# Layer 3 of a hybrid network on one core: attention, two norms and gate logits as one pipeline of four-tile groups

## The chip, the cores and the metric

The kernel runs on one core of a Trainium2 chip. The metric is the device time of one execution in microseconds (us). Over 10 runs the kernel before took a median of 14244.46 us (14234.97 to 14262.62).

The engines are named as in the profile: PE multiplies matrices (PEld loads its stationary operand), DVE is the vector engine, ACT the scalar engine with its function tables, POOL the GpSimd engine, SP the engine that issues most of the transfers. Each engine executes its own queue in order; SP and ACT also issue transfers, in the same queue as their other work.

## The reference, cut to what matters

The network has four layers on an input of 2 x 64 x 64 x 128 (8192 tokens of 128 channels, in float32). Layers 0 to 2 (selective scan, deformable convolution, gated scan with a spectral convolution) aren't touched. Layer 3 is, with x of shape (2, 4096, 128):

```python
# attention, on the layer-normed x
h = layernorm(x)
q = exp(h @ Wq + bq); k = exp(h @ Wk + bk); v = h @ Wv + bv
x = x + q @ (k.T @ v)                    # one 128 x 128 product per batch entry
# mixture of experts, experts choose tokens
n = layernorm(x)
logits = n @ gate_w.T + gate_b           # 64 experts
p = softmax(logits over the tokens)      # per batch entry and expert
g = p where it is among the 8 largest of its row, else 0
xw = g.T @ n                             # one mixed token per batch entry and expert
y = gelu(xw @ weight1 + b1) @ weight2 + b2
x = x + g @ y
```

It is written here as the kernel computes it; what matters is the order: one norm, an attention whose 128 x 128 product needs all the tokens of a batch entry, a second norm, logits, a softmax and a choice of eight over all 4096 tokens, the experts' two large weights (64 x 128 x 512 each, 16.8 MB apiece), and the result added to x.

## The kernel before

The tokens lie in `X`, 64 tiles of 128 tokens (partitions) by 128 channels; each of the two batch entries has 32 tiles (`NTB`). Layer 2 writes its result to HBM, and `move` (L1691) loads it into `X` in eight transfers. Then `layer3a` and `layer3f` run, one after the other.

`layer3a` does for each batch entry:
- `layernorm` (L99): `bn_stats` and `bn_aggr` for 32 tiles on DVE (L107, L108); one reciprocal square root for all 32 (`rsqrt`, L77: a square root on ACT at L82 and six small DVE operations); then tile by tile the normalised copy, in turn on DVE (L121) and ACT (L119), and its transpose on PE into PSUM (L95), copied to `xt` by DVE (L72) and ACT (L74) in turn.
- `pq` (L1529) and its exponential into `qt` (L1530), `pkv` (L1535) with bias (L1537) and exponential (L1538), the product `kvp` over all tiles (L1540) and its copy `kvs` (L1542).
- `po` (L1546), added to `X` (L1548).

`layer3f` loads the first four pieces of the experts' first weight (`w1`, L1569, 2 MB each, on SP's queue), normalises `X` a second time into a copy `xn3` of its own, transposes it, and forms the logits of both batch entries as the sum of two zero-padded products in one PSUM tile (L1592), so that partition 64 b + e holds expert e of batch entry b. The whole row of 4096 logits is then searched for its eight largest values (`max`, L1595), these are overwritten (`match_replace`, L1596), the exponential and its sum are taken (L1600), and in eight pieces the chosen places are found (L1604) and the weighted values put into `G` (L1605). `G` is transposed (L95) into `gt`, and `pp` (L1612) forms the mixed tokens, copied to `xw` (L1613). Only after that are `b1`, `b2`, `sel8` and `sel2` loaded, on ACT's queue (L1617 to L1624), and on SP's queue the first three pieces of the second weight (`w2`). The expert loop goes over eight groups of eight experts: `ph` (L1644), a copy, `phid` with the selector `sel8` (L1648), bias and GELU (L1650, L1652), `pout` with `w2` (L1657), `poe` with the selector `sel2` (L1663). The last part multiplies by `G` (`py`, L1675), adds `X` (L1677) and stores.

The order of each engine's queue in layer 3 isn't written out: the framework's planner sorts the instructions, by the order in which they are written and by the time at which it believes their operands ready, so that work of the second batch entry can slip between work of the first. (Layer 2 has an order written by hand.) A buffer is reused when all its readers are done; a new pool lies where an earlier one lay, and its first writers wait for that memory's last readers.

Of the kernel before, what the change touches and what calls it, by code (L numbers as in the profile page):

```python
# [96 lines left out]


def layernorm(k, pool, ps, t0, n, tag, xn=None, xt=None):  # L99


    nc = k.nc
    st = pool.tile([P, n, 6], F32, name=f"{tag}_st", tag=f"{tag}_st")
    mv = pool.tile([P, n, 2], F32, name=f"{tag}_mv", tag=f"{tag}_mv")
    rs = pool.tile([P, n], F32, name=f"{tag}_rs", tag=f"{tag}_rs")
    for i in range(n):
        nc.vector.bn_stats(st[:, i, :], k.X[:, t0 + i, :])  # L107
        nc.vector.bn_aggr(mv[:, i, :], st[:, i, :])  # L108
    rsqrt(nc, pool, rs, mv[:, :, 1], 1e-5, [P, n], tag)
    sh = pool.tile([P, n], F32, name=f"{tag}_sh", tag=f"{tag}_sh")  # L110
    nc.vector.scalar_tensor_tensor(sh, mv[:, :, 0], -1.0, rs, ALU.mult, ALU.mult)

    def normalised(i):
        if xn is not None:
            o = xn[:, i, :]
        else:
            o = pool.tile([P, C], F32, name=f"{tag}_n", tag=f"{tag}_n", bufs=6)
        if i % 2:
            nc.scalar.activation(o, k.X[:, t0 + i, :], AF.Identity, bias=sh[:, i : i + 1], scale=rs[:, i : i + 1])  # L119
        else:  # L120
            nc.vector.tensor_scalar(o, k.X[:, t0 + i, :], mv[:, i, 0:1], rs[:, i : i + 1], ALU.subtract, ALU.mult)  # L121
        return o

    if xt is None:
        for i in range(n):
            normalised(i)
    else:
        to_channels(k, ps, xt, normalised, n)
# [1379 lines left out]
def layer3a(k):  # L1508
    tc, nc, ins, X = k.tc, k.nc, k.ins, k.X
    with ExitStack() as es:  # L1510
        enter = es.enter_context
        cst = enter(tc.tile_pool(name="a3c", bufs=1))
        pool = enter(tc.tile_pool(name="a3p", bufs=2))
        wk = enter(tc.tile_pool(name="a3w", bufs=4))
        ps = enter(tc.tile_pool(name="a3ps", bufs=6, space=PSUM))
        pk = enter(tc.tile_pool(name="a3pk", bufs=2, space=PSUM))
        wq = cst.tile([P, C], F32, name="wq")
        nc.sync.dma_start(out=wq, in_=ins["wq3"])
        wkv = cst.tile([P, 2, C], F32, name="wkv")
        nc.sync.dma_start(out=wkv[:, 0, :], in_=ins["wk3"])  # L1520
        nc.sync.dma_start(out=wkv[:, 1, :], in_=ins["wv3"])
        for b in range(B):
            xt = pool.tile([P, L], F32, name="xt3")
            layernorm(k, pool, ps, b * NTB, NTB, "ln3", xt=xt)
            qt = pool.tile([P, L], F32, name="qt")
            for q in range(8):
                s = slice(q * N, (q + 1) * N)
                pq = ps.tile([P, N], F32, name="pq3", tag="ps")
                nc.tensor.matmul(pq, wq, xt[:, s], start=True, stop=True)  # L1529
                nc.scalar.activation(qt[:, s], pq, AF.Exp, bias=k.v("bq"))  # L1530
            kvp = pk.tile([P, C], F32, name="kvp")
            for i in range(0, NTB, 2):
                pkv = ps.tile([P, 2, 2 * C], F32, name="pkv", tag="ps")
                for j in range(2):
                    nc.tensor.matmul(pkv[:, j, :], xt[:, (i + j) * P : (i + j + 1) * P], wkv.rearrange("p a c -> p (a c)"), start=True, stop=True)  # L1535
                kv = wk.tile([P, 2, 2 * C], F32, name="kv")
# [12 lines left out]

def layer3f(k, out):


# [307 lines left out]
```

## Time and profile before

| | us |
|---|---|
| median of 10 runs | 14244.46 |
| the profiled execution, its own time | 14250.63 |
| its span | 14248.9 |
| layer 3: first `bn_stats` to the end of the span | 13945.7 to 14248.9 |
| of this: first `bn_stats` to the first transposition | 13945.7 to 13958.4 |
| first `kvs` to second `kvs` | 13996.9 to 14043.1 |
| last logits out of PSUM | 14084.0 |
| `pp`, 128 matmuls | 14109.7 to 14137.1 |
| wait of PE for `sel8` | 14143.8 to 14153.8 |
| `py` | 14230.0 to 14244.5 |

The profile's time for one execution lies 6.17 us above the median of the runs, so times read from the profile are used as differences. Over the whole span the page has DVE busy for 90%, POOL for 86%, PE for 81% and ACT for 64%; almost all of that is layers 0 to 2. In layer 3 no engine is busy throughout, and each stage has another limit, so the tables by stage say more than the page's shares. "PEclk" is the clock that PE was granted, 1.00 being full speed.

### The profile page before, as it was taken

To read this page: it belongs to the slowest core of one execution; us is meant where nothing else is said; L and a number is where in the kernel's file an instruction comes from. 1 tells how busy PE (TensorE), PEld (TensorE's weight loads), DVE (VectorE), ACT (ScalarE), POOL (GpSimd) and SP (SyncE) were. 2 spreads that over 40 slices of the span, in tenths; PEclk is the share of its full clock that TensorE was granted. 3 is DMA by queue.
4 is the path that set the end of the run, shared out by engine and by line. 5 is a ranking of instruction groups with operands and counts; after the bars stand their busy time and mean duration, and the time that the engine had idled before them with its cause. 6 is when DMAs were issued, how large, how long until landed. Compare 5 with 4: busy or idle time off the path is not lost. (4 is left out here: it accounts for less than half of the span.)

```text
span 14248.9 us, 234505 instructions
## 1 busy us (share of the span) xinstructions
PE 11537.0 (81%) x91784; PEld 7492.7 (53%) x91784; DVE 12780.6 (90%) x11825; ACT 9132.5 (64%) x15238; POOL 12199.8 (86%) x3232
## 2 busy tenths in 40 slices
PE   7888788887895464979869798797887989989997
PEld 4444544445883132646536465564454656656665
DVE  7889678896658999999999999999999999999953
ACT  5777367772115676777767667667777777777742
POOL 5888358882778999999999999999999999999950
PEclk9999799998996676989879899898998999999998
DMA  7999679996974454656656565565665666666653
GB/s 180 228 226 231 174 169 230 229 230 172 285 213 153 151 175 155 214 186 206 196 172 206 187 203 202 191 204 187 205 202 185 208 196 206 208 199 205 210 150 133
DMA packets 1388836, 2800.92 MB, mean 197 GB/s; under 512 B 375985, under 2 KB 1046353, under 8 KB 1184721
## 3 DMA queue, kind: packets, MB, share of 16 engines
q1 hardware_dynamic: 1192560, 1556.57, 41.5%
q10 hardware_dynamic: 148608, 1076.17, 20.9%
q0 software_dynamic: 46560, 153.18, 3.6%
q8 instruction: 724, 11.86, 0.4%
q14 instruction: 384, 3.14, 0.1%
HBM read 2364.15 MB, written 421.31 MB: 195 GB/s over the span
## 5 line engine op out<-in xcount | busy, mean ns | idle before, releaser
L1462 DVE TENSOR_TENSOR_SCAN S<-dA,S 128x512 f32<-128x512 f32 x8192 | 9155.0, 1195 | 123.4 <-ACT dA L1460 97.5
L1406 POOL TENSOR_TENSOR S<-row,g 128x4088 f32<-128x4088 f32 (+1 forms) x1024 | 9058.9, 8897 | 182.8 <-DMA row<-drow 114.4
L1460 ACT ACTIVATE dA<-row,a_t 128x512 f32<-128x512 f32 x8192 | 5632.2, 692 | 2491.3 <-DVE S L1462 2396.1
L1425 PE MATMUL Z<-S,cv 128*32 128x256 f32 x32768 | 2568.1, 445 | 1633.1 <-ACT ze L1430 1288.2
L1264 PE MATMUL pef<-hk,ur 128*128 128x256 f32 x14336 | 3550.6, 388 | 18.4 <-DMA hk<-in_phi_dram 12.7
L1264 PEld LDWEIGHTS pef<-hk,ur 128*128 128x128 f32 x14336 | 2630.1, 191 | 973.1 <-issue 628.6
L404 POOL TENSOR_TENSOR S<-row,bt 128x2048 f32<-128x2048 f32 x512 | 2318.4, 4529 | 353.4 <-DMA row<-drow 285.4
L1425 PEld LDWEIGHTS Z<-S,cv 128*32 128x32 f32 x32768 | 1029.7, 123 | 2873.2 <-issue 1411.0
L502 DVE TENSOR_TENSOR_SCAN S<-dA,S 128x1024 f32<-128x1024 f32 x1024 | 2282.6, 2272 | 100.4 <-POOL S L410 82.6
L424 PE MATMUL dA<-dt,quad 64*128 64x255 f32 x8192 | 1251.8, 431 | 420.9 <-DVE S L502 379.6
L438 ACT ACTIVATE dA<-dA 128x1020 f32<-128x1020 f32 x1024 | 1022.5, 1003 | 344.8 <-PE dA L424 280.7
L424 PEld LDWEIGHTS dA<-dt,quad 64*128 64x128 f32 x8192 | 784.0, 203 | 868.9 <-DVE S L502 525.4
L1264 PEld LDWEIGHTS pef<-hd,ur 128*128 128x128 f32 x4096 | 752.2, 191 | 302.6 <-issue 196.0
L1264 PE MATMUL pef<-hd,ur 128*128 128x256 f32 (+1 forms) x4096 | 861.6, 335 | 5.8 <-ACT e L1244 3.1
L1236 PE MATMUL acc<-e,mw 128*128 128x512 f32 x1600 | 855.9, 618 | 5.6 <-ACT e L1244 4.5
L779 POOL DMA_INDIRECT G<-table,idx x576 | 553.9, 962 | 219.0 <-issue 141.3
L456 PE MATMUL Z<-S,W 128*32 128x128 f32 x16384 | 658.7, 294 | 101.4 <-ACT ze L462 87.8
L1430 ACT COPY ze<-Z 128x512 f32<-128x512 f32 x1024 | 591.6, 578 | 166.1 <-PE Z L1425 135.6
L456 PEld LDWEIGHTS Z<-S,W 128*32 128x32 f32 x16384 | 432.2, 116 | 393.8 <-issue 187.7
L787 DVE TENSOR_TENSOR G<-G,wv 128x1536 f32<-128x1536 f32 x192 | 335.9, 1751 | 271.2 <-DMA G<-table,idx 254.7
L1244 ACT COPY e<-pef 128x512 f32<-128x512 f32 x800 | 464.7, 581 | 167.9 <-PE acc L1236 106.1
L791 PE MATMUL pv<-ident,G 128*128 128x128 f32 x4608 | 534.7, 278 | 2.8 <-DVE G L787 2.8
(344 smaller groups left out, 7407.0 us busy)
## 6 DMA issues: line engine op xcount, KB each, us to landing
row<-drow ACTq DMA_DIRECT2D x1024, 1024.0 KB, 5.4
row<-drow SPq DMA_DIRECT2D x512, 1024.0 KB, 12.7
zd<-ze SPq DMA_DIRECT2D x1024, 256.0 KB, 2.7
hk<-in_phi_dram SPq DMA_DIRECT2D x224, 320.5 KB, 4.4
hk<-in_phi_dram SPq DMA_DIRECT2D x160, 448.5 KB, 5.1
hd<-in_phi_dram SPq DMA_DIRECT2D x512, 128.5 KB, 4.4
hk<-in_phi_dram SPq DMA_DIRECT2D x96, 576.5 KB, 6.1
mw<-wdr SPq DMA_DIRECT2D x400, 128.0 KB, 3.1
```

Of the source, the lines that this page charges most:

```text
L404: nc.gpsimd.tensor_tensor(S[:, o, :], rows.pop(s), bt[:, 0, sub * T : (sub + 1) * T].unsqueeze(1).to_broadcast([P, 8, T]), ALU.mult)
L424: nc.tensor.matmul(dA[:, 2 * a + h, rest], stats[d, j][r, h, :], dt[r, h, at : at + T - 1], start=True, stop=True)
L438: nc.scalar.activation(dA[:, :, rest], dA[:, :, rest], AF.Exp)
L456: nc.tensor.matmul(Z[32 * q : 32 * q + 32, :, :, a].rearrange("p t g -> p g t"), w, S[:, :, t : t + 4], start=True, stop=True)
L502: nc.vector.tensor_tensor_scan(flat, dflat, flat, 0.0, ALU.mult, ALU.add)
L1236: nc.tensor.matmul(box["acc"].rearrange("p a s -> p (a s)"), ms[f][:, o, :], e, start=box["first"], stop="whole" in box and (f, o) == todo ...
L1264: nc.tensor.matmul(pe[:, a, 256 - n :], ur[:, par, j, :], h[:, at : at + n], start=i == 0, stop=i + 1 == len(mm))
L1406: nc.gpsimd.tensor_tensor(S, row[:, :, first:].unsqueeze(1).to_broadcast([P, 2, R, T - first]), g[:, :, first:].unsqueeze(2).to_broadcast( ...
L1425: nc.tensor.matmul(Z[32 * j : 32 * j + 32, q].rearrange("p t e -> p e t"), cv[:, h, s], S[:, h, :, s], start=h == 0, stop=h == 1)
L1430: nc.scalar.copy(ze, Z)
L1460: nc.scalar.activation(dA, row[:, j % R, :], AF.Exp, scale=a_t[:, h, d : d + 1])
L1462: nc.vector.tensor_tensor_scan(s, dA, s, 0.0, ALU.mult, ALU.add)
```

## The change

`layer3a`, `layer3f` and the helper `layernorm` are replaced by one function `layer3`, called in their place.

- Statistics are taken for a group of four tiles (`stats`): four `bn_stats` and four `bn_aggr` on DVE, and the reciprocal square root by fourteen operations on POOL with one exponential of the bit pattern on ACT between the first and the second, in place of the square root on ACT and six DVE operations for 32 tiles. `mv3` and `vs3` keep mean, rsqrt, square root and shift of all 64 tiles for one norm at a time.
- `transposed` normalises and transposes one group; all copies out of PSUM are ACT's. The first norm, `pq`, `pkv` and `kvp` follow group by group, with `kvp` one group behind.
- The second norm is written over `X` itself, group by group behind `po`; the copy `xn3` is gone. The first batch entry's transposed tiles are kept in `G`'s memory. POOL undoes the norm in the expert loop (`X = X * sqrt(var) + mean`, one operation a tile).
- Logits use two groups of 64 columns of PE, one for each batch entry, in place of two padded products that are added. They and a `max` of each group of 512 follow the transposes of the second batch entry.
- The exponential (ACT) is issued beside `match_replace` (DVE); marking and weighting are one operation a piece, without the sum; the reciprocal of the sum goes into the matrix `big_r` by which `G` is transposed (a float32 matmul, no longer a transposition), and into `oe`.
- `b1`, `b2`, `sel8` and the gate weight are loaded at the start of the layer, on ACT's queue, with the attention's weights. `w1`'s four pieces are loaded during the first batch entry. `sel2` is loaded behind the first three pieces of `w2`.

```diff
+def layer3(k, out):
+    NE, EG, HF, Q = 64, 8, 512, 4
+    NQ = NTB // Q
...
+        wq = cst.tile([P, C], F32, name="wq")
+        nc.scalar.dma_start(out=wq, in_=ins["wq3"])
...
+        gw = cst.tile([P, NE], F32, name="gw")
+        nc.scalar.dma_start(out=gw, in_=ins["gate_w"])
...
+        sel8 = cst.tile([P, 8], F32, name="sel8")
+        nc.scalar.dma_start(out=sel8, in_=ins["sel8"])
+        big_r = cst.tile([P, P], F32, name="big_r")
+        mv = cst.tile([P, NT, 2], F32, name="mv3")
+        vs = cst.tile([P, NT, 4], F32, name="vs3")
+        w1 = {}
         with ExitStack() as e2:
             pre = e2.enter_context(tc.tile_pool(name="m3p", bufs=1))
+            wk = e2.enter_context(tc.tile_pool(name="m3wk", bufs=4))
             ps = e2.enter_context(tc.tile_pool(name="m3ps", bufs=6, space=PSUM))
+            pa = e2.enter_context(tc.tile_pool(name="m3pa", bufs=2, space=PSUM))
+            def stats(q):
+                st = wk.tile([P, Q, 6], F32, name="st3")
+                i = slice(q * Q, q * Q + Q)
+                for j in range(Q):
+                    nc.vector.bn_stats(st[:, j, :], X[:, q * Q + j, :])
+                for j in range(Q):
+                    nc.vector.bn_aggr(mv[:, q * Q + j, :], st[:, j, :])
+                va, r, t, m = (vs[:, i, n] for n in range(4))
+                g = nc.gpsimd
+                g.tensor_scalar(va, mv[:, i, 1], 1e-5, None, ALU.add)
+                nc.scalar.activation(r, va.bitcast(I32), AF.Exp, scale=-0.5 * LN2 / 2**23, bias=root[:, 0:1])
+                g.tensor_tensor(t, va, r, ALU.mult)
+                g.tensor_tensor(t, t, r, ALU.mult)
+                g.tensor_scalar(m, t, 0.375, -1.25, ALU.mult, ALU.add)
+                g.tensor_tensor(m, t, m, ALU.mult)
+                g.tensor_scalar(m, m, 1.875, None, ALU.add)
+                g.tensor_tensor(r, r, m, ALU.mult)
+                g.tensor_tensor(t, va, r, ALU.mult)
+                g.tensor_tensor(t, t, r, ALU.mult)
+                g.tensor_scalar(t, t, -0.5, 1.5, ALU.mult, ALU.add)
+                g.tensor_tensor(r, r, t, ALU.mult)
+                g.tensor_tensor(m, mv[:, i, 0], r, ALU.mult)
+                g.tensor_scalar(m, m, -1.0, None, ALU.mult)
+                g.tensor_tensor(t, va, r, ALU.mult)
+            def transposed(q, keep, out):
+                pt = ps.tile([P, N], F32, name="pt", tag="ps")
+                for j in range(Q):
+                    i = q * Q + j
+                    o = X[:, i, :] if keep else wk.tile([P, C], F32, name="xn3", bufs=6)
+                    if j % 2:
+                        nc.vector.tensor_scalar(o, X[:, i, :], mv[:, i, 0:1], vs[:, i, 1:2], ALU.subtract, ALU.mult)
+                    else:
+                        nc.scalar.activation(o, X[:, i, :], AF.Identity, bias=vs[:, i, 3:4], scale=vs[:, i, 1:2])
+                    nc.tensor.transpose(pt[:, j * P : (j + 1) * P], o, k.ident)
+                nc.scalar.copy(out, pt)
+            lg = pre.tile([P, L], F32, name="lg")
+            G = cst.tile([P, L], F32, name="G3")
+            xt4 = G
+            m64 = pre.tile([P, NQ, 8], F32, name="m64")
+            def logits(q, xt):
+                pl = ps.tile([P, N], F32, name="pl", tag="ps")
+                for b, t in enumerate((xt4[:, q * N : (q + 1) * N], xt)):
+                    nc.tensor.matmul(pl[b * NE : (b + 1) * NE, :], gw, t, start=True, stop=True)
+                s = lg[:, q * N : (q + 1) * N]
+                nc.scalar.activation(s, pl, AF.Identity, bias=k.v("gate_b"))
+                nc.vector.max(m64[:, q, :], s)
             for b in range(B):
+                at = b * NQ
+                qt = pre.tile([P, L], F32, name="qt", tag="big", bufs=2)
+                kvp = pa.tile([P, C], F32, name="kvp")
+                behind = []
+                def products():
+                    while behind:
+                        q, j, kv = behind.pop(0)
+                        for h in range(2):
+                            nc.tensor.matmul(kvp, kv[:, h, :C], kv[:, h, C:], start=q == j == h == 0, stop=q == NQ - 1 and j == h == 1)
+                stats(at)
+                for q in range(NQ):
+                    if q + 1 < NQ:
+                        stats(at + q + 1)
+                    xt = wk.tile([P, N], F32, name="xt3")
+                    transposed(at + q, False, xt)
+                    pq = ps.tile([P, N], F32, name="pq3", tag="ps")
+                    nc.tensor.matmul(pq, wq, xt, start=True, stop=True)
+                    nc.scalar.activation(qt[:, q * N : (q + 1) * N], pq, AF.Exp, bias=k.v("bq"))
+                    products()
+                    for j in range(2):
+                        pkv = ps.tile([P, 2, 2 * C], F32, name="pkv", tag="ps")
+                        for h in range(2):
+                            s = slice((2 * j + h) * P, (2 * j + h + 1) * P)
+                            nc.tensor.matmul(pkv[:, h, :], xt[:, s], wkv.rearrange("p a c -> p (a c)"), start=True, stop=True)
+                        kv = wk.tile([P, 2, 2 * C], F32, name="kv")
+                        nc.vector.tensor_tensor(kv, pkv, k.r("bkv").unsqueeze(1).to_broadcast([P, 2, 2 * C]), ALU.add)
+                        nc.scalar.activation(kv[:, :, :C], kv[:, :, :C], AF.Exp)
+                        behind.append((q, j, kv))
+                    if b == 0:
+                        w1[q // 2] = w1.get(q // 2) or load(wp1, "w1", q // 2)
+                products()
+                kvs = wk.tile([P, C], F32, name="kvs", bufs=2)
+                nc.vector.tensor_copy(kvs, kvp)
+                def normalised(q):
+                    if b == 0:
+                        transposed(at + q, True, xt4[:, q * N : (q + 1) * N])
+                    else:
+                        xt = wk.tile([P, N], F32, name="xt3")
+                        transposed(at + q, True, xt)
+                        logits(q, xt)
+                for q in range(NQ):
+                    po = ps.tile([P, N], F32, name="po4", tag="ps")
+                    for j in range(Q):
+                        i = q * Q + j
+                        nc.tensor.matmul(po[:, j * P : (j + 1) * P], qt[:, i * P : (i + 1) * P], kvs, start=True, stop=True)
+                    o = X[:, (at + q) * Q : (at + q + 1) * Q, :]
+                    nc.vector.tensor_tensor(o, po.rearrange("p (a c) -> p a c", c=C), o, ALU.add)
+                    stats(at + q)
+                    if q > 0:
+                        normalised(q - 1)
+                normalised(NQ - 1)
+            m8 = pre.tile([P, 8], F32, name="m8")
+            nc.vector.max(m8, m64.rearrange("p a b -> p (a b)"))
+            sm = cst.tile([P, 4], F32, name="sm3")
+            nc.vector.tensor_scalar(sm[:, 0:1], m8[:, 0:1], -1.0, None, ALU.mult)
+            ex = pre.tile([P, L], F32, name="ex", tag="big", bufs=2)
+            nc.scalar.activation(ex, lg, AF.Exp, bias=sm[:, 0:1], accum_out=sm[:, 1:2])
+            nc.vector.match_replace(G, m8, lg, -3.0e38)
+            nc.vector.reciprocal(sm[:, 2:3], sm[:, 1:2])
+            nc.vector.tensor_scalar(big_r, k.ident, sm[:, 2:3], None, ALU.mult)
+            gt = pre.tile([P, NTB, P], F32, name="gt", tag="big", bufs=2)
+            pp = pa.tile([P, P], F32, name="pp", tag="kvp")
+            for q in range(NQ):
                 s = slice(q * N, (q + 1) * N)
+                nc.vector.scalar_tensor_tensor(G[:, s], G[:, s], -3.0e38, ex[:, s], ALU.is_equal, ALU.mult)
+                pt = ps.tile([P, N], F32, name="pt", tag="ps")
+                for j in range(Q):
+                    i = q * Q + j
+                    nc.tensor.matmul(pt[:, j * P : (j + 1) * P], G[:, i * P : (i + 1) * P], big_r, start=True, stop=True)
+                nc.scalar.copy(gt[:, q * Q : q * Q + Q, :], pt.rearrange("p (a c) -> p a c", c=P))
             for b in range(B):
                 for i in range(NTB):
+                    nc.tensor.matmul(pp[:, b * NE : (b + 1) * NE], X[:, b * NTB + i, :], gt[:, i, b * NE : (b + 1) * NE], start=i == 0, stop=i == NTB - 1)
             nc.vector.tensor_copy(xw[:, :, 0:B], pp.rearrange("p (b e) -> p e b", b=B))
...
         w2 = {g: load(wp2, "w2", g) for g in range(3)}
+        sel2 = cst2.tile([P, NE // 4, P], F32, name="sel2")
+        nc.scalar.dma_start(out=sel2, in_=ins["sel2"])
         for g in range(NE // EG):
...
             hid = wk.tile([P, EG, 4, B], F32, name="hid")
             nc.vector.tensor_tensor(hid, ph, b1[:, g * EG : (g + 1) * EG].unsqueeze(3).to_broadcast([P, EG, 4, B]), ALU.add)
+            for i in range(g * EG, (g + 1) * EG):
+                nc.gpsimd.tensor_scalar(X[:, i, :], X[:, i, :], vs[:, i, 2:3], mv[:, i, 0:1], ALU.mult, ALU.add)
             h = hz[g % 2]
             nc.scalar.activation(h[:, :, :, 0:B], hid, AF.Gelu)
...
             nc.vector.tensor_tensor(oe[s, b, :], poe[s, :], b2[s, :], ALU.add)
+            nc.vector.tensor_scalar(oe[s, b, :], oe[s, b, :], sm[s, 2:3], None, ALU.mult)
...
             if "3a" in stages:
-                layer3a(k)
-            if "3f" in stages:
-                layer3f(k, out)
+                layer3(k, out)
```

The lines of `layernorm`, `layer3a` and `layer3f` that these replace are printed above.

## The prediction

> **What bounds the kernel now.** The page shows layers 0 to 2 filling the first 97% of the span; nothing there changes. I cut layer 3 into stages at the ends of its steps and asked for busy time by stage (columns: stretch, its length, then PE, PEld, DVE, ACT, POOL busy with counts, PE's clock, transfer share, GB/s):
>
> ```profile
> 13945.50:13997.00 51.50, 36.64 (x176) 26.17 (x176) 37.04 (x182) 26.64 (x53) 0.00 (x0) 0.84 0.04 11
> 13997.00:14043.30 46.30, 42.31 (x240) 32.52 (x240) 35.87 (x130) 27.38 (x60) 0.00 (x0) 1.00 0.00 1
> 14043.30:14084.00 40.70, 30.99 (x160) 21.77 (x160) 24.32 (x104) 17.65 (x34) 1.80 (x1) 0.87 0.50 207
> 14084.00:14098.30 14.30, 0.00 (x0) 0.00 (x0) 9.03 (x5) 5.08 (x3) 0.00 (x0) 0.64 0.00 0
> 14098.30:14109.70 11.40, 7.53 (x32) 6.45 (x33) 11.40 (x20) 1.76 (x3) 0.00 (x0) 0.50 0.01 1
> 14109.70:14137.50 27.80, 27.44 (x130) 27.25 (x128) 1.46 (x4) 0.59 (x1) 0.17 (x1) 0.50 0.00 1
> 14137.50:14168.00 30.50, 20.33 (x82) 9.53 (x86) 2.56 (x6) 2.97 (x5) 1.93 (x3) 0.56 0.77 317
> 14168.00:14229.90 61.90, 53.77 (x722) 37.97 (x714) 6.76 (x16) 6.34 (x16) 0.00 (x0) 0.87 0.66 272
> 14229.90:14248.90 19.00, 14.56 (x128) 14.37 (x128) 11.38 (x18) 0.00 (x0) 0.00 (x0) 0.99 0.74 222
> ```
>
> Three stages of attention, second norm and logits (138.5 us), in which PE already works 110 us and POOL nothing; the search for the largest logits (14.3); marking (11.4); `pp` (27.8, PE at half clock); the experts (92.4); the output. The chain of waits then says what is late in the middle:
>
> ```profile
> 14084.03 4.44 DVE m L1595
> 14088.49 4.49 DVE G L1596 x2
> 14093.12 1.28 ACT L1600
> 14094.41 3.81 ACT ex L1600 x2
> ...
> 14109.94 27.21 PE pp L1612 x128
> 14138.09 15.71 DMA sel<-in_sel_dram
> ```
>
> Search, overwriting, table load and exponential stand in a row; and 4 KB of `sel8`, asked for behind 6 MB of `w2`, take 15.71 us to land. A finer cut of the transfers shows what follows:
>
> ```profile
> 14158.00:14162.00 4.00, 4.00 (x13) 2.31 (x14) 0.55 (x2) 1.54 (x2) 0.00 (x0) 0.50 0.79 338
> 14162.00:14166.00 4.00, 4.00 (x21) 3.05 (x25) 0.22 (x1) 0.26 (x1) 0.00 (x0) 0.50 0.02 4
> 14166.00:14170.00 4.00, 4.00 (x48) 2.18 (x44) 0.69 (x1) 0.59 (x1) 0.00 (x0) 0.50 0.00 0
> ```
>
> Nothing moves for some 10 us: `w2`'s fourth piece waits for a buffer, that for the first `pout`, that for `phid` and `sel8`. The experts are bound by transfers, with a hole in them.
>
> The new norm's operations occur in layer 2 in the same form, among the groups by line:
>
> ```profile
> L1138 POOL TENSOR_TENSOR vf<-vf 128x4 f32<-128x4 f32 x16 | 3.2, 202 | 1.2
> L1133 POOL TENSOR_SCALAR vf<-vf 128x4 f32<-128x4 f32 x16 | 3.6, 226 | 1.4
> ```
>
> 202 to 230 ns each, and 1.2 to 1.4 us of idleness per 16: 0.08 us for an operation that waits for the one before it.
>
> **1. Attention to logits: -12 us.** POOL gets 32 groups of 14 operations. In a chain that waits for itself an operation takes 0.206 + 0.08 = 0.285, a group 4.0 and all 128 us; with two groups' chains interleaved a group takes 2.9, all 92. The planner interleaves: in the trace it put second-entry `bn_stats` between the dependent steps of the first `rsqrt` on DVE. I take 2.9, the other end stays in the range. PE, per group of the first norm, from the timeline's pitches: transposes 4 x 0.116, `pq` 2 x 0.43, `pkv` 8 x 0.217, `kvp` 8 x 0.11: 3.94; of the second: `po` 8 x 0.116 and transposes, 1.39. DVE (four statistics at 0.26, two norms, two biases) and ACT (two norms, copy, three exponentials) stay near 2.9.
> Start as before, 13945.7. First group: statistics 1.2, POOL and exponential 0.8, thirteen operations 3.7 to 5.4, a norm: PE starts near 13953.5 (before 13958.4). Then PE has 31.5 + 11.1 + 31.5 = 74 us up to the second `kvs`; at the density of the second stage (42.3 of 46.3) 81, plus 3 at half clock and 2.5 around the first `kvs`: 14040 (before 14043.1). Behind it `po`, addition and statistics 2.9, eight groups on POOL 23.2 (DVE has as much: addition 0.6, statistics 1.04, norms 0.55, `max` 0.69 by the 512-wide rows), then norm, transposes, copy, logits (0.86 if the column groups overlap as `ph`'s four do, else 1.7) and their copy, 3.6; with 2 for two queues as full as each other 32: 14072, before 14084. The eight table loads of 1.283 outside GELU vanish within this and the next part. Ends: -20 if PE runs dense, +2 if POOL's chains never interleave (13946.9 + 96 + 3.5 to the second `kvs`, then 2.9 + 32 + 3.6).
> The Trainium skill speaks against this part: "GPSIMD Engine Reference", section "Performance versus the Vector engine", has a two-input operation at 1.96 times DVE's time. At this size the rows disagree (POOL 202 ns, DVE's L85 185 ns); by the rule, 448 operations at twice 0.185 would be 166 us, and this part about +37 instead of -12.
>
> ACT's seven small loads (0.33 to 0.54 us each to issue, some 3.2) stand ahead of the first exponential. The memory's last transfer ends at 13945.3, so the exponential, due at 13947.2, may be 1.3 late; inside the ends. `w1`'s 8 MB now land under the attention, where the transfer share is 0.04; before they landed under the second norm, also hidden: nothing.
>
> **2. Search: -8.5 us.** The 4096-wide `max` (4.4) becomes one last 512-wide (0.69) and one of 64 (0.2); negation 0.14; then `match_replace` 4.5 covers the exponential (3.7 + 0.19), whose table load is gone. With 0.2 of handing over 5.8 against 14.3.
>
> **3. Marking and `pp`: -0.6 us.** A piece costs DVE 0.66 instead of 1.26, so PE becomes this stage's limit: 64 float32 matmuls (two passes each of 32) for 32 transpositions. Reciprocal, `big_r` and first piece 1.3; then at half clock 64 x 0.24 = 15.4, at full clock 64 x 0.116 = 7.4. PE has been idle for 8 us, and in the trace 3 to 6 us of dense work bring the clock back (0.50, 0.86, 1.00 in successive 3 us from 13958): 9.5. 10.8 against 11.4; ends -2.7 and +5.3. `pp` keeps its 128 matmuls at 0.214: 27.4.
> The row to weigh: `pp` keeps PE busy for 27.4 us and is granted 0.50 throughout, and before it come idle 17 us. The Trainium skill, "TensorE: Matmul & The Clock Gate", section "What's actually happening", lets about 3.4 us of sustained activity lift the clock; by that `pp` would have sped up, which it did not. By the rule alone, with PE warm from the matmuls ahead, `pp` would take 13.7 and this part -14.3. I follow the row: 64 columns behind each load of 128 don't count as dense.
>
> **4. Experts: -22 us.** From `xw` on, 12 pieces of 2.1 MB and `sel2` (1 MB) have to come: 26.2 MB at the 425 GB/s of the full windows (412 to 438), 61.7 us. `phid` waits no more; the first `w2` lands in 8 us (shortest landing 7.2), so the fourth is asked for at about 11, while the first five transfers last 22: no hole. With 2 to start and a tail of 4.7 (`pout`, copy, `poe`, `oe`) 68.4 against 92.4. The added wait is `poe`'s for `sel2`: asked for behind `w2` it lands, as `sel8` did, some 16 us on, and PE's later `phid`, `ph` and `pout` queue behind it for up to 7 us. Transfers have 32 us of work by then, so it is covered, but I leave 2 for it: -22, ends -17 and -28 (a piece of `w2` or `sel2` whose memory is free earlier).
> POOL's 64 restorations cost 0.60 each (L526, L527, same form: 602 to 604): 38.6 and `hz`'s 1.9, done long before `py`. The cover is the experts' 70 us; at twice the price 11 would stick out.
>
> **5. Output: +0.5 us.** Two more steps on `oe` at 0.29.
>
> Sum: -12 - 8.5 - 0.6 - 22 + 0.5 = -42.6. The profiled execution (14250.63) becomes 14208.0; the median, 6.2 lower, 14201.9: 14202.
>
> **The rivals.**
> *POOL's chains don't interleave* (ends of part 1 at 2, or at +11 to +26 when each chain also waits 0.5 to 1 us for its exponential): -28.6 to -4.6, 14216 to 14240. For it: the order is the planner's guess, and ACT's queue is strict. Against: many groups' statistics are ready at once.
> *PE stays warm through `pp`*: another -13.7, 14188. Against it stands the row above.
> *POOL's pace sets the layer, and it ends slower.* One mechanism: small POOL operations are held up beside DVE, which here does norms and `bn_stats` all the time; the rows of layer 2 stand beside long scans only. The point: parts 2 to 5 give 30.6, so slower by over 0.2% (28.5 us, about what a measurement of this kernel can tell from no change) needs attention to last 197 us, 6.1 per group, 0.43 per operation. At 0.57, twice the chain's pitch, 32 x 8 = 256 us: +86 in all, 14331. In layer 2 the same rows vary only from 195 to 232 ns: unlikely.
> *The wait moves to `sel2` uncovered*: 7 dearer, 14209.
>
> **How the numbers follow.** The forecast with its ends 0.60; not interleaved 0.23; `pp` warm 0.12; slow POOL 0.05. Faster by more than 28.5: all of the first and the third, hardly any of the second, 0.72; within, 0.23; slower 0.05. For 8 in 10 the range reaches to 14180 (warm, or the favourable ends of parts 1 and 4) and to 14232, most of the second case.
>
> **What would show it.** Right: POOL's operations 0.2 apart, second `kvs` by 14040, last logits by 14072, exponential inside `match_replace`, `pp` at 27 us and 0.50, no hole in the transfers after `xw`. Wrong: gaps of POOL on ACT's exponential, PE waiting for norms all along, `pp` at 14 us, PE held at `poe` for `sel2`, or `py` waiting for POOL.

## The result, and the profile after

The changed kernel takes 14306.23 us (median of 8 runs, 14289.98 to 14311.57); beside them on the same chip the kernel before takes 14252.00 (28 runs). The ratio is 1.0037, 95% interval 1.0028 to 1.0046: slower by some 54 us, where the forecast was 14202 in a range of 14180 to 14232.

The profiled execution has a span of 14299.3 us against 14248.9. From the end of layer 2's last DVE operation I measured in both traces:

| stretch of layer 3 | before, us | after, us | change | forecast |
|---|---|---|---|---|
| layer 2's end to last logits copied | 141.0 | 219.3 | +78.3 | -12 |
| to the last transposed piece of `G` (search, marking) | 26.9 | 16.7 | -10.2 | -9.1 |
| `pp` | 26.3 | 13.6 | -12.7 | 0 |
| `xw` to `oe` (experts) | 92.4 | 77.7 | -14.7 | -22 |
| `oe` to the last addition | 15.6 | 18.0 | +2.4 | +0.5 |
| sum | 302.2 | 345.3 | +43.1 | -42.6 |

Layer 2 ends 7.7 us later (13943.00 and 13950.70) and the last stores take 0.4 less, which makes up the rest of the 50.4 us between the spans. Layers 0 to 2 issue the same instructions in the same order in both kernels, and in the four profiles of the first experiments below, which ran together on one chip, that point lies between 13931.0 and 13955.1. So I compare stretches of layer 3 rather than single totals.

Busy time by stage of the changed kernel (columns as in the prediction: PE, PEld, DVE, ACT, POOL busy, PE's clock, transfer share, GB/s):

```profile
13953.30:14011.10 57.80, 38.16 (x176) 27.44 (x176) 20.81 (x81) 23.57 (x56) 21.77 (x113) 0.80 0.40 162
14011.10:14060.00 48.90, 20.09 (x96) 17.05 (x96) 23.93 (x120) 14.42 (x35) 26.81 (x129) 0.67 0.00 1
14060.00:14107.90 47.90, 40.73 (x176) 28.94 (x176) 19.46 (x68) 22.59 (x54) 19.27 (x96) 0.88 0.00 1
14107.90:14170.00 62.10, 38.29 (x128) 16.29 (x128) 24.17 (x96) 18.63 (x40) 23.45 (x112) 0.76 0.00 1
...
14176.60:14185.90 9.30, 9.27 (x64) 9.30 (x65) 4.10 (x7) 4.10 (x7) 0.00 (x0) 0.76 0.01 2
14185.90:14200.40 14.50, 14.43 (x130) 14.29 (x128) 0.04 (x1) 0.59 (x1) 14.03 (x33) 1.00 0.00 1
14200.40:14279.10 78.70, 68.10 (x800) 44.10 (x800) 10.21 (x25) 9.32 (x21) 15.70 (x35) 0.87 0.80 334
```

The first four rows are first norm and attention, then second norm, of the first batch entry, and the same of the second. They stand one after another; the search (6.6 us) is left out. In row three PE is busy for 40.73 of 47.9 us (before: 42.31 of 46.3). In rows two and four no engine is busy for more than 62% of the time: not throughput, but waiting. DVE in the second row, from the timeline (brackets: idle time ahead, and what ended it):

```profile
14018.12 0.60 DVE L1553 TENSOR_SCALAR X<-X,mv,vs 128x128 f32<-128x128 f32 x2 [1.80 <-POOL vs L1541]
14022.45 0.60 DVE L1553 TENSOR_SCALAR X<-X,mv,vs 128x128 f32<-128x128 f32 x2 [3.73 <-POOL vs L1541]
14022.97 0.68 DVE L1626 TENSOR_TENSOR X<-po,X 128x512 f32<-128x512 f32 x1
...
14029.00 0.60 DVE L1553 TENSOR_SCALAR X<-X,mv,vs 128x128 f32<-128x128 f32 x2 [0.55 <-POOL vs L1541]
```

And POOL at the same place:

```profile
14014.64 0.23 POOL L1530 TENSOR_SCALAR vs<-mv 128x4 f32<-128x4 f32 x1 [35.16 <-DVE mv L1527]
14015.28 0.20 POOL L1532 TENSOR_TENSOR vs<-vs 128x4 f32<-128x4 f32 x1 [0.42 <-ACT vs L1531]
14015.57 0.20 POOL L1533 TENSOR_TENSOR vs<-vs 128x4 f32<-128x4 f32 x1
...
14018.89 0.23 POOL L1530 TENSOR_SCALAR vs<-mv 128x4 f32<-128x4 f32 x1
```

An operation lasts 0.20 but they start 0.285 apart, each waiting for the one before; the next group's chain starts only when this one is through, 4.25 us later (14014.64, 14018.89). DVE's queue then holds the next two groups' additions (L1626) behind two norms that wait for these chains (14018.12 and 14022.45), so the next pair's statistics come only afterwards, and a pair takes 10.9 us (14018.12 to 14029.00). In the fourth row a pair takes 13.3 and more (norms at 14114.88 and 14128.18), as a `max` that waits for the logits stands in the same queue. POOL had been idle for 35.16 us before: it had served the first norm's eight groups, whose chains do interleave, in 26 us, and the second norm could begin only when the attention was done.

From there on the chain of waits reads (some of its pieces):

```profile
14171.17 4.39 DVE G L1638
14176.64 9.45 PE pt L1649 x64
14186.08 9.34 PE pp L1653 x84
...
14213.63 1.79 POOL hz L1659 x2
```

The exponential is gone from the chain, `pp` runs at full clock, and a new name stands in it: `hz`.

### The profile page after: what moved, and what is told of

Same layout as the page of the kernel before. It is cut to its first block, busy times and chain, and to the rows that moved or that the text cites. A ratio compares the mean times of both kernels' runs of the same rounds, so it can differ in the third digit from the quotient of the medians.

```text
span 14299.3 us, 235146 instructions
## 1 busy us (share of the span) xinstructions
PE 11546.1 (81%) x91816; PEld 7488.0 (52%) x91816; DVE 12765.6 (89%) x11781; ACT 9142.1 (64%) x15278; POOL 12322.2 (86%) x3743
```

## The experiments

Three things needed a cause: the four stretches in a row, `pp`'s clock, and the experts' missing 7 us. `hybrid`, `wide_all`, `pause_before_pp` and `before_warmed` ran on a chip on which the kernel before takes 14408.77; their totals are compared with that alone. It takes 14248.28 beside `both_first`, `wide8`, `look3_only` and `hz_early`, and 14237.80 beside `chain_on_dve`, `merged` and the repetition of `hybrid`. Lengths below count from layer 2's end, so the changed kernel's own is 219.3 to the last logits (the expectations count 216.7 from layer 3's first operation).

**The order of writing: `both_first`.**

```diff
+            kept = []
             for b in range(B):
...
                 nc.vector.tensor_copy(kvs, kvp)
+                kept.append((qt, kvs))
+            for b in range(B):
+                at = b * NQ
+                qt, kvs = kept[b]
 
                 def normalised(q):
```

> Only the order in which layer 3 is written changes: first norm and attention of both batch entries, then both second norms (as in the kernel before). The changed kernel's start-to-last-logits stretch is 216.7 us (57.8 first entry's norm and attention, 48.9 its second norm, 47.9 second entry's norm and attention, 62.1 its second norm and logits); the kernel before needs 138.3. Theory of the chains (16 second-norm groups each wait for 14 dependent POOL operations, 4.2 us, one group after the other): the second norms keep their pace, only the second entry's first norm gains by starting under the first entry: 190 to 212 us, time 14280 to 14302. Theory of the order (the second entry's first norm takes its buffers behind the first entry's second norm, and that alone takes the overlap away): 150 us or less, time 14240 or less.

Measured: 14286.86 us, ratio to the kernel before 1.0035 (1.0021 to 1.0050); 218.7 to the last logits. Busy time by stage (first entry's attention; second entry's; both second norms):

```profile
13931.00:14007.20 76.20, 43.19 (x183) 31.02 (x184) 30.38 (x151) 28.21 (x71) 42.99 (x225) 0.77 0.31 127
14007.20:14043.10 35.90, 35.03 (x182) 26.55 (x181) 14.70 (x29) 18.73 (x42) 0.00 (x0) 1.00 0.01 1
14043.10:14149.70 106.60, 59.12 (x215) 34.56 (x214) 42.60 (x184) 32.01 (x72) 46.63 (x224) 0.68 0.00 0
```

The second entry's statistics and all its chains (225 POOL operations instead of 113) now run under the first entry, and the second attention is dense (PE 35.03 of 35.9). But that costs the first entry 15.8 us (76.2 against 60.4), and the sixteen second-norm groups take 6.7 us each. The second `kvs` now comes 112.1 us behind layer 2's end, but the stretch is as long as before, longer than either theory expected: the lost overlap by itself is not what costs, it is where the cost shows.

**Fewer, wider chains: `wide8`.**

```diff
-            def stats(q):
+            def stats(q, n=1):
...
-                    stats(at + q)
-                    if q > 0:
-                        normalised(q - 1)
-                normalised(NQ - 1)
+                    if q % 2 == 0:
+                        continue
+                    stats(at + q - 1, 2)
+                    for p in (q - 3, q - 2):
+                        if p >= 0:
+                            normalised(p)
+                normalised(NQ - 2)
+                normalised(NQ - 1)
```

> Second norms' statistics and POOL chain over eight tiles instead of four, two groups of four then normalised behind each; all else as in the changed kernel. A pair of groups now takes two chains of 4.2 and a gap of 2.4 us (first entry) or 5.4 (second). Theory of the chains: an operation on eight columns costs POOL what one on four does, so a pair takes one chain and its gap: the first entry's second norm falls from 48.9 to about 30, the second's from 62.1 to about 43, the stretch from 216.7 to about 179, time about 14268. Theory of the order: the chains are not the limit, gain under 8 us. Theory of POOL's throughput (time goes by columns): no gain in the chains either, the same.

Measured: 14268.13 us, ratio 1.0014 (1.0004 to 1.0023); 191.3 to the last logits. First entry's attention; its second norm and the second entry's attention; second entry's second norm:

```profile
13954.70:14030.60 75.90, 43.94 (x176) 31.71 (x176) 30.00 (x150) 26.78 (x67) 42.61 (x225) 0.71 0.31 127
14030.60:14101.30 70.70, 54.83 (x272) 41.87 (x272) 32.61 (x118) 32.66 (x73) 12.33 (x56) 0.86 0.00 1
14101.30:14146.00 44.70, 33.39 (x129) 16.21 (x128) 22.87 (x96) 17.21 (x36) 12.15 (x56) 0.85 0.00 1
```

From the first `kvs` to the second entry's first transposition it is 30.0 us instead of 48.9, and the last row is 44.7 instead of 62.1: 36.3 us from halving the chains of two second norms, against 38 priced, since an operation on eight columns costs POOL 0.207 us and one on four 0.203. The second attention takes 40.8 instead of 47.9 because, as in `both_first`, its chains are drawn forward, and the first row pays 15.5 for that. So the stretch is 28.0 us shorter, not 38. That the total fell by the 38 expected is luck: 5.1 come from the experts, 1.7 from the last stretch, and the kernel before was itself 3.7 faster here.

**Statistics further ahead: `look3_only`.**

```diff
 (LOOK, which is 3, written out)
-                    if q > 0:
-                        normalised(q - 1)
-                normalised(NQ - 1)
+                    if q >= 3:
+                        normalised(q - 3)
+                for q in range(NQ - 3, NQ):
+                    normalised(q)
```

> In the second norms, group q is normalised after the statistics of group q+3 are written instead of q+1, so DVE's queue has the additions and statistics of three groups ahead of a norm that waits for POOL; the chains stay as they are. Theory of the chains with gaps: the gaps close (2.4 and 5.4 us per pair), the chains remain: second norms about 40 us each instead of 48.9 and 62.1, stretch about 187, time about 14276. Theory of the order alone: no gain (under 5 us). If the chains interleave once statistics lie ready, as in the first entry's first norm (POOL's 8 groups in 26 us): second norms about 30 each, stretch 167, time 14256.

Measured: 14278.52 us, ratio 1.0022 (1.0012 to 1.0032); 198.4 to the last logits, 20.9 less. The second norms, the first one counted to the second entry's first transposition, take 44.2 and 46.9 us instead of 48.9 and 62.1; about 40 each were expected. So the gaps, and not only the chains, cost, and the chains do not begin to interleave by having statistics ready: in the first entry they start 4.4 apart on average, where interleaved ones would be at 2.9 to 3.3.

**The engine: `chain_on_dve`.**

```diff
-                g = nc.gpsimd
+                g = nc.vector
```

> The changed kernel with the 13 POOL operations of every chain given to DVE (one word: the engine); the exponential stays on ACT, hz is still late. DVE's dependent small operations stand 0.2 us apart in the kernel before's first rsqrt, POOL's 0.285: a chain takes about 3.2 us instead of 4.2, but in DVE's own queue, beside 2.5 us of additions, statistics and norms per group. Theory of the serial chains: a pair of second-norm groups takes 10 to 11 us as before in the first entry and 12 in the second, the first norms 46 to 55: layer 2's end to last logits 195 to 215 us instead of 219, time within 25 us below the changed kernel's. Rival, it is POOL (its dispatch and the semaphores to it) and not the chain's length and order that costs: 160 us or less.

Measured: 14259.10 us, ratio 1.0016 (1.0006 to 1.0025); 190.6 to the last logits, just under the first theory's range. Counted as for `look3_only`, the second norms take 41.1 and 53.2 instead of 48.9 and 62.1; the first attention is 4.8 shorter and the second 7.2. An operation lasts 0.16 and dependent ones start 0.2 apart; here the planner does put two groups' chains into each other (they start 1.6 apart, at 14009.22 and 14010.85). A better place for the chain, but the stretch is still 50 us longer than the kernel before's.

**Wide chains everywhere: `wide_all`, then `merged`.** `wide_all`:

```diff
 (the loops as in both_first, hz cleared before the search, and:)
-                stats(at)
                 for q in range(NQ):
-                    if q + 1 < NQ:
-                        stats(at + q + 1)
+                stats(at, 1); stats(at + 1, 3); stats(at + 4, 4)
...
-                    stats(at + q)
-                    if q > 0:
-                        normalised(q - 1)
+                    if q == 1: stats(at, 2)
+                    elif q == 4: stats(at + 2, 3); normalised(0); normalised(1)
+                    elif q == 7: stats(at + 5, 3); (normalised(2) to normalised(7))
```

> The changed kernel with first norms of both entries ahead of both second norms, hz cleared before the search, and POOL's chain run over 4, 12 and 16 tiles in the first norm and 8, 12 and 12 in the second: 12 chains instead of 32, everything else kept (X in place, restored later). Theory of the chains: 20 chains of 4.2 to 4.9 us fall away, the entries overlap again: layer 2's end to last logits 140 to 160 us instead of 219, experts 74, time about 14229 (14219 to 14240). Rival, POOL's or ACT's handovers in themselves (an exponential in the middle of every chain, in order behind ACT's other work): 180 us or more, time 14260 or more.

Measured: 14407.61 against 14408.77 us, ratio 0.9998 (0.9989 to 1.0007); 161.1 to the last logits, just above the 140 to 160 expected; the total, expected 12 to 33 us below the kernel before's, is level with it. The second attention ends at 93.5 (kernel before 100.1), and then two second norms stand in a row, 29 and 39 us: the second entry's first `po` comes only behind the first entry's norms, which are written ahead of it. That it waits for PSUM buffers that they hold is my reading; it was not told apart from their place in PE's queue. `merged` changes both:

```diff
 (attention, added - po, addition, statistics of 16 tiles after every fourth group -
  and normalised are generators that yield after each group; drain takes turns)
+            drain(attention(0))
+            drain(attention(1), added(0))
+            drain(added(1), normalised(0))
+            drain(normalised(1))
```

> As wide_all (10 chains in all: 4, 12 and 16 tiles wide in the first norm, 16 in the second), but the first entry's additions and statistics are written group by group beside the second entry's attention, and its norms beside the second entry's additions, so that no po waits for a PSUM buffer that a norm still holds. wide_all took 161 from layer 2's end to the last logits (second kvs at 93.5, then two second norms in a row, 29 and 39); hybrid 136.5. If that row is what wide_all loses: second kvs at about 100, last logits at 128 to 145, layer 3 about 256, beside hybrid's 259: the same time as hybrid within what can be measured. Rival, X in place and POOL's chains cost by themselves: 155 or more, 15 us or more above hybrid.

Measured: 14207.20 us beside 14237.80 of the kernel before, ratio 0.9980 (0.9971 to 0.9989); second `kvs` at 100.6, last logits at 140.9. The pipeline with the norm in place, written so that chains are few and the second norms no longer stand in a row, is as fast as the kernel before's attention (141.0), no faster.

**Without the pipeline: `hybrid`.** The kernel before with the second half of the change.

```diff
 (layer3a, layernorm and xn3 stay; in layer3f:)
+        (gw, b1, b2, sel8 loaded on SP's queue ahead of w1; sel2 behind w2)
-                    nc.tensor.matmul(pl, gw[:, b, :], xts[b][:, s], start=b == 0, stop=b == B - 1)
+                    nc.tensor.matmul(pl[b * NE : (b + 1) * NE, :], gw, xts[b][:, s], start=True, stop=True)
+                nc.vector.max(m64[:, q, :], lg[:, s])
...
 (from the search to gt, and the division in oe, as in the changed kernel)
```

> The kernel before with only the second half of the change: attention, both norms (statistics of a whole batch entry, on DVE, second norm into its own copy) stay; logits in two column groups with a maximum per 512, exponential beside the overwriting, marking and transposition by matmul with big_r, small weights loaded early, sel2 behind w2, the division moved to oe; no restoration of X, since X is not overwritten. Measured lengths: kernel before, from layer 2's end to the last logits 141, search and marking 26.9, pp 26.3, experts 92.4; changed kernel 219, 16.7, 13.6, 77.7 (73.8 with hz_early). Theory: the second half's gains do not depend on the pipeline, so 141 + 16.7 + 13.6 + 74 + 16.3: 41 us less than before, time about 14211 (14205 to 14218). Rival: pp is fast only because of what the pipeline leaves in front of it; then pp stays 26 to 27 us and the time is about 14224.

Measured: 14378.82 against 14408.77 us, ratio 0.9977 (0.9968 to 0.9986). 136.5, 17.3, 13.7, 73.9 and 18.0 for the five stretches, 259.4 in all. Layer 3 is as long as expected and `pp` fast without the pipeline, but the total is 30 us lower, not 41. It was run once more beside `merged`:

> The same kernel as hybrid, on the same chip as merged: 259 us of layer 3, 30 to 40 us below the kernel before (ratio 0.9972 to 0.9979).

Measured: 14207.21 against 14237.80, ratio 0.9980 (0.9970 to 0.9989); 135.5, 18.1, 13.7, 68.3, 18.0. `hybrid` and `merged` beat both kernels, the kernel before by some 30 us. The profiles show 43 to 49 less in layer 3. The other 13 to 18 I cannot locate: as with the changed kernel (54 in the medians, 43 in layer 3), the medians stand 11 to 18 us higher than layer 3 alone explains in nine of the ten comparisons (in `both_first` 2 lower), with layers 0 to 2 in the same order. What all ten share is the one profile of the kernel before; the next experiments give a reason to doubt its `pp`.

**`pp`'s clock, from both sides: `pause_before_pp` and `before_warmed`.**

```diff
 (changed kernel)                          (kernel before)
+for _ in range(3):                      +for q in range(16):
+    nc.vector.tensor_copy(gt, gt)       +    pt = ps.tile([P, N], F32, name="pt", tag="ps")
 (pp)                                    +    for j in range(4):
                                         +        nc.tensor.matmul(pt[:, j * P : (j + 1) * P], gt[:, NTB - 1, :], k.ident, ...)
                                          (pp)
```

> The changed kernel with three copies of gt onto itself on DVE put between the last transposition and pp, so that TensorE rests for about 10 us ahead of pp (in the changed kernel pp follows 64 matmuls at once, runs at full clock and takes 14.4 us; in the kernel before it follows idleness and sparse transposes, is granted 0.50 and takes 27.4). Theory, pp keeps the clock it finds: it starts cold and takes 25 to 28 us at 0.50. Rival, pp's own operands decide: 14.4 us again. Third: the clock comes back after 3 to 4 us of pp: 15 to 18 us.

> The kernel before with 64 matmuls (128 columns, float32, result unused) put directly ahead of pp; nothing else changed. Theory, pp keeps the clock it finds: the added matmuls take 9 to 12 us and bring the clock up, pp takes 14 us at full clock instead of 27.4; the time is about 1 to 4 us lower than before's. Rival, pp's own operands decide: pp 27 us, and the time is 9 to 15 us higher.

Measured, one profile each. With the pause, by windows (the end of the transposition, a stretch of `pp`):

```profile
14330.00:14334.00 4.00, 4.00 (x38) 4.00 (x38) 0.00 (x0) 2.77 (x5) 0.00 (x0) 1.00 0.00 0
14350.00:14360.00 10.00, 10.00 (x49) 10.00 (x48) 0.00 (x0) 0.00 (x0) 10.00 (x25) 0.50 0.01 2
```

The transposition had brought the clock to 1.00; 7.7 us of rest took it away; `pp`, the same instructions on the same operands, then took 27.57 us, busy throughout at 0.50. In the kernel before with matmuls ahead, `pp`'s last 118 matmuls took 13.29 us at 1.00 (ten had slipped ahead of the added ones). So `pp` holds the clock that it finds, and did not raise it in 27 us. `before_warmed` as a whole took 14414.63 us, beside a median of 14408.77: a single run that says nothing on the gain; `pp` and the added matmuls together filled 27.5 us.

But the added matmuls are not what brought the clock there. They begin at 14271.01, and ahead of them stand:

```profile
14268.00:14271.00 3.00, 2.64 (x18) 2.67 (x19) 3.00 (x6) 0.98 (x2) 0.00 (x0) 0.70 0.00 0
14269.95 1.23 PE L1616 MATMUL pp<-gt,xn 128*128 128x64 f32 x10
```

The clock stood at 0.50 up to 14269 and at 1.00 from 14270, and the ten matmuls of `pp` took 0.12 each, where the kernel before's take 0.214. The 32 transpositions ahead of them are the same, at the same spacing, in both profiles: in one execution they lifted the clock, in the other they did not. So `pp` need not be cold in every execution of the kernel before. Where it is warm, its layer 3 is some 13 us shorter than the profile's 302.2, about what is missing above. That is a guess: it takes more profiles of the kernel before.

**`hz` out of the way: `hz_early`.**

```diff
+        hz = [cst.tile([P, EG, 4, 32], F32, name=f"hz{i}") for i in range(2)]
...
+            for h in hz:
+                nc.gpsimd.memset(h, 0.0)
             m8 = pre.tile([P, 8], F32, name="m8")
...
-        hz = [cst2.tile([P, EG, 4, 32], F32, name=f"hz{i}") for i in range(2)]
-        for h in hz:
-            nc.gpsimd.memset(h, 0.0)
         wp2 = enter(tc.tile_pool(name="m3w2", bufs=3))
```

> The two clearings of hz are written before the search for the largest logits, so they no longer stand in POOL's queue behind the restorations of X. Theory of the queue: GELU's 6.35 us of waiting for hz go, the first pout comes about 9 us after xw instead of 17.7, and the experts fall from 78.5 us to about 70: time about 14298. Theory of the transfers (26 MB of weights at 425 GB/s set the stage): under 2 us of gain.

Measured: 14299.14 us, ratio 1.0037 (1.0023 to 1.0051), which is not to be told from the changed kernel; `xw` to `oe` 73.8 instead of 77.7, first `pout` 15.6 us behind `xw` instead of 17.7. In the changed kernel POOL's queue had, just ahead of the clearing at 14213.50:

```profile
14186.37 27.26 POOL L1685 TENSOR_SCALAR X<-X,vs,mv 128x128 f32<-128x128 f32 x63 [24.72 <-PE pp L1653]
```

and ACT's GELU:

```profile
14214.55 0.26 ACT L1687 ACTIVATE hz<-hid 128x64 f32<-128x64 f32 x1 [6.35 <-POOL hz L1659]
```

The wait went, most of the expected gain did not come, and of the kernels that still clear `hz` late three (`wide8`, `look3_only`, `chain_on_dve`) take 72.6 to 74.3 and one (`both_first`) 77.5, each with a wait of 6.1 to 6.2 us. So `hz` is worth between nothing and 4 us. Transfers set the stage: in all these kernels the weights come without a hole, as here in the changed kernel and in `hybrid_again`:

```profile
14220.40:14262.00 41.60, 36.40 (x481) 25.13 (x474) 4.94 (x11) 4.07 (x11) 0.00 (x0) 0.87 1.01 427
14262.00:14266.00 4.00, 4.00 (x13) 0.83 (x12) 0.00 (x0) 0.59 (x1) 0.00 (x0) 0.50 0.33 139
```

```profile
14110.00:14166.00 56.00, 49.40 (x638) 30.47 (x632) 7.22 (x17) 8.80 (x19) 0.00 (x0) 1.00 1.01 427
14166.00:14170.00 4.00, 2.94 (x72) 2.65 (x72) 1.09 (x3) 0.26 (x1) 0.00 (x0) 1.00 0.86 365
```

The rate is the same 427 GB/s; what differs is how long PE works on behind the last weight: some 15 us with its clock down to 0.50, some 5 at 1.00. Of the eight kernels, those with a lower mean clock in this stage broadly have the longer one: 68.3 at 1.00, 70.2 at 0.95 (`merged`), 72.6 to 74.3 at 0.93 to 0.88, 77.5 and 77.7 at 0.87. What lowers the clock in some of these runs was not tried.

## Why the prediction was wrong, by its steps

**Part 1 is the step that failed, by 90 us** (-12 forecast, +78 measured). Against the kernel before the first attention lost 6.5 us, the second 1.7 and the two second norms with the logits 70.1: they stand alone for 48.9 and 62.1, where the kernel before, whose first `po` lies under the second attention, has 40.9 behind its second `kvs`. The prediction took 2.9 us per group from chains that interleave, because "the planner interleaves". It does so where many groups' statistics are ready at once: the first entry's first norm, eight groups in 26 us. (Even there the first group pays for it: among five chains its own took 9.0 us, and PE began 14.1 us behind layer 3's first operation, not 7.8.) In the sixteen groups of the second norms it does not: 4.25 us each. The second entry's first norm lies between: its chains start 3.9 us apart on average and are through at 14086.1, 22 us before the second `kvs`; from then on PE sets the pace. That chains might not interleave was foreseen as a rival, and the rival's price (+2 to +26) was just as wrong, since both summed POOL's busy time and let the rest lie beside it; to being slower by what came the prediction gave 0.05. What the runs show in its place is a loop through in-order queues: statistics and addition (DVE), the chain with an exponential in it (POOL, ACT, POOL), the norm (DVE, ahead of the next additions), and only then the next pair of groups. In the second norms a chain's latency is paid in full, 16 times, with 2.4 to 5 us of handing over for every pair. Halving these chains gave 36.3 us in the norms and 28.0 in the stretch (`wide8`), more distance 20.9 (`look3_only`), few chains and another order of writing together 78 (`merged`). The second wrong term is the overlap of the two entries: the 74 us of PE's work up to the second `kvs`, which held 11.1 for the first entry's second norm, were taken at the density of the kernel before, where that norm comes behind the second attention. Here it stands between the two attentions for 48.9 us, and the second `kvs` came 157 us behind layer 2's end instead of 100. Moving it back behind alone (`both_first`) gained 0.6.

On POOL's speed the forecast held: 203 ns alone, 0.285 us from one to the next in a chain, no contention with DVE (thirteen of the chain's fourteen rows have means of 201 to 233 ns in layer 3, beside norms and statistics, and one 275), so the rival of a slow POOL fell although its total was nearest. The Trainium skill's "GPSIMD Engine Reference", section "Performance versus the Vector engine", which was weighed against this part, would again have missed by its ratio, which that page measures at 2048 columns: `chain_on_dve` has 151 to 165 ns for what POOL does in about 203, 1.3 times and not 1.96. DVE's row in the prediction (L85, 185 ns) was of 32 columns; on 4 columns the same line takes 162 ns in the kernel before. The page pointed to the right engine all the same.

**Part 2 held**: 6.6 us up to the first transposition against 7.1 (5.8, and 1.3 of part 3), with the exponential inside the overwriting.

**Part 3: transposition 9.45 against 9.5; `pp` was the other way.** The prediction read 0.50 as a property of `pp`. Its own step had the clock up at the end of the transposition, and did not ask what `pp` would do with it. The runs show the same `pp` at 0.50 behind a rest (27.57 us) and at 1.00 behind dense work (14.40). The -12.7 of the table holds for the profile of the kernel before; where its `pp` runs warm, as `before_warmed` suggests it can, there is nothing to gain here. The Trainium skill's "TensorE: Matmul & The Clock Gate", section "What's actually happening", has some 3.4 us of activity lift the clock, and as much idleness lower it. The trace agrees for the changed kernel's transposition (0.50, 0.67 and 1.00 in successive windows of 2.4, 3.0 and 3.9 us from 14176.6) and for the pause (1.00 up to 14339, some 5 us into the rest, 0.50 from 14340); it does not for a cold `pp`, 27.57 us busy without a rise. What about `pp` the gate does not count as activity (64 columns behind a load of 128, or another thing) was not separated.

**Part 4: -14.7 for -22.** The wait for `sel8` and the hole in the transfers are gone, the 61.7 us of transfers are there, and no wait of `poe` for `sel2` appears. The mis-sized term is the tail, 4.7 at full clock; with the clock low it was some 15. At 1.00 throughout, `hybrid_again` takes 68.3, the 68.4 of the forecast. Overlooked was `hz`'s clearing behind 63 restorations in POOL's queue: 6.35 us of waiting for GELU, of which up to 4 reach the end. The restorations themselves follow each other by 0.433, not 0.60, and cost nothing on the path: `hz_early` with them and `hybrid` without take 73.8 and 73.9.

**Part 5**: +2.4 for +0.5; `py` ran at 0.92 instead of 0.99 of the clock (16.2 us instead of 14.6), and it did so in `hybrid` too. In six other runs (`merged` among them) it took 14.5 and the stretch 16.3, +0.7: the two steps on `oe` were priced about right, and why `py`'s clock varies is open.

## What to carry to other kernels

A short chain of small dependent operations that crosses engines is priced by its latency times the number of chains that can't overlap, not by its busy time; before believing that they overlap, look in each in-order queue for what stands behind the consumer of a chain. Where the chain works on a few columns, make it wider and rarer, or it will decide the loop. And when an edit changes what runs ahead of a stage, carry the clock over the seam: a stage's duration in the old trace includes the clock it was handed.

## What was not expected of the hardware

- A stage of matmuls with 64 columns behind loads of 128 stayed at 0.50 for 27.57 us while PE was busy all the time, and stayed at 1.00 for 14.4 us when it found the clock there. Ahead of it, the same 32 transpositions at the same spacing raised the clock in one profile (`before_warmed`) and left it at 0.50 in another (the kernel before).
- POOL's small operations hardly ask how wide they are: 0.203 us on 4 columns, 0.207 on 8, 0.222 on 16. Dependent ones start 0.285 apart, independent ones 0.15, less than an operation's own duration.
- The same instructions of layers 0 to 2 end up to 24 us apart from one kernel's profile to the next on one chip (13931.0 to 13955.1), more than most of the effects studied here; totals of single runs could not have told them apart.
